# The end of a graph layer on one Trainium2 core: row products split between VectorE and TensorE, eight PSUM banks in two rings, and weights prepared at the start

## The chip, the core and the metric

The kernel runs on one core of a Trainium2 chip. A core has TensorE (matrix products into PSUM, a memory of eight banks), VectorE, ScalarE and GpSimd (work along rows of 128 partitions), SyncE (which issues loads here), and DMA engines that move data between HBM and SBUF. Each engine takes its instructions in order from a queue of its own. The metric is the device time of one execution in microseconds; less is better. Tables of the profile call TensorE PE (PEld where it loads weights), VectorE DVE, ScalarE ACT, GpSimd POOL and SyncE SP.

## The reference, cut to what matters

Four layers follow each other, each with a normalisation. x is 3327 x 64, adj 3327 x 3327. The change touches the end of layer 1 and what it hands to layer 2.

```python
x = _layernorm(x + L0(t, x, adj))        # layer 0
x = _layernorm(x + L1(x, adj, att_W))    # layer 1, in a ball (hyperbolic)
x = _layernorm(x + L2(x, adj, W))        # layer 2
x = _layernorm(x + L3(x, adj, weight, bias))

# layer 1
left, right = x_tan @ att_W[:D] + att_b, x_tan @ att_W[D:]
adj_att = sigmoid(left + right.T) * adj
support = einsum('ij,ijd->id', adj_att, _logmap(x[:, None], x[None, :]))
return _proj(_expmap(x, support))        # per node: norms, tanh, two scalings

# layer 2, twice
agg = adj @ x
x = tanh(concatenate([agg, x], 1) @ W[k])
```

The sum over j in layer 1 can be written as a vector m (a weighted sum of rows of x) and a scalar t (a sum of weights) for each node. What comes after it needs, for each node, three numbers besides scalars that are known early: p, the row product of m with x; q, the squared length of the centred m; and t. The node's result is alpha times m plus beta times x, with alpha and beta worked out from p, q, t by some fifty operations on a tile of 128 x 26 scalars. The product of layer 2 with its first weights is linear, so it is formed as alpha (m W) + beta (x W) once alpha and beta are there.

## The kernel before, in words

Nodes are padded to 26 blocks of 128. A tile "128 x 26" holds one scalar for each node. Columns of nodes are kept turned, two halves of 13 blocks stacked on the 128 partitions (64 features each): `mT` and `ljT` are such tiles of 128 x 1664, and one block of 128 columns stands for two blocks of nodes. Most of the kernel's instructions have an order written out by hand for each engine.

**Beginning (L104 to L300).** SyncE issues the loads in program order: x, the attention weights, two adjacency blocks that stay in SBUF (`keep`, L142 to L146), and then six small loads: layer 2's weights in two halves into `w2_dg`, layer 3's into `w3_dg`, a bias and the attention weights again (L156 to L165). Layer 0 is reduced to a centring and a scaling. In L1267 to L1279 TensorE forms the attention products; after the first and the last group of them a product with no reader (`idle`, L1277) fills its time. ScalarE loads its tables for square root and sigmoid (L1280, L1281).

**Layer 1's loop (`near_sphere`, L1302).** 104 tiles go through products on TensorE (L1400), an arctangent on ScalarE (L1409), two weightings on VectorE (L1420 to L1424), a sigmoid on ScalarE (L1373) times adjacency on GpSimd (L1378), and a product that sums over j into two banks (L1444). ScalarE copies the sums to `mT` (L1450). Before the last tiles end, GpSimd forms the first half of `xm`, the elementwise product of `mT` with the turned rows of x (L1627), and six tiles of scalars (L1630 to L1635); TensorE turns and centres the first six column blocks of `mT` (`pq_early`, L1640), and ScalarE squares them into `sq_e` and copies their t (L1645, L1649). After the loop VectorE makes three tiles of scalars (L1652 to L1654), the other half of `xm` (L1656) and the first 12 of q (L1657).

**Layer 1's end (`near_end`, L1659).** PSUM is divided into a ring of four banks (`l1w`), one bank for p (`l1t`) and a ring of three (`l1m`). TensorE turns and centres the other seven column blocks (`m_and_t`, L1711), then forms p for all 13 blocks as products of `xm` with two columns of ones (`pe`, L1735). ScalarE squares (L1729), VectorE sums (L1773, L1774). ScalarE copies the centred m to `x2` (`m_out`). VectorE works through the scalars: k, gp, u2, th; ScalarE takes tanh (L1819) and loads the table for square roots (L1822); VectorE goes on to `root`, ScalarE takes a root, VectorE goes to `var`, ScalarE takes the second root (L1852, twice); then alpha and beta (L1883, L1884). Meanwhile TensorE works out two weight tiles, `w_x` and `w_m` (L1786 to L1798), turns and centres the first six column blocks a second time, and forms x W (`times(..., w_x, ...)`) and m W (`times(..., w_m, ...)`). Both weight tiles are the centred layer 2 weights with two rows set to zero: `w_x` is made as rows times (center W), `w_m` as (rows times center) W. VectorE combines them into `lj` in five groups (L1890 to L1892), writes the last scalar `beta_c` (shown by the profile as `gsp`, L1893), and finishes `x2` (L1897 to L1899).

**Into layer 2 (L485 to L640).** Loads for it are issued by SyncE in program order: three more kept blocks (L2103) and four stream blocks (L218) before `near_end`, as their buffers come free; then, inside the layer, one block into a buffer `bt` that lies where layer 1's end had its tiles, and further stream blocks. TensorE multiplies `lj` with the adjacency blocks (L517), in the order: four stream blocks, a kept one, `bt`, stream blocks, and so on.

Of the kernel before, what the change touches and what calls it, by code (L numbers as in the profile page):

```python
# [10 lines left out]
F32 = mybir.dt.float32  # L11
# [3 lines left out]
AF = mybir.ActivationFunctionType  # L15
ALU = mybir.AluOpType
# [66 lines left out]
def kernel(  # L83
# [62 lines left out]
    keep((NB - 1, NB - 2))  # L146

# [9 lines left out]
    with nc.allow_non_contiguous_dma(reason="two short columns"):  # L157
# [7 lines left out]
        nc.sync.dma_start(attw_sb, att_w.rearrange("(t d) o -> d (t o)", d=D))  # L165

# [136 lines left out]

    def layer_3_constants():
        nc.gpsimd.tensor_scalar(w3_dg, w3_dg, float(2**27), None, ALU.mult)

    def centred_weights(ps):

        pw = ps.tile([P, P], F32, name="pw_3")
        nc.tensor.matmul(pw, center, w3_dg, start=True, stop=True)  # L310
        nc.scalar.copy(w3_dg, pw)

# [877 lines left out]
    with tc.tile_pool(name="l1", bufs=1) as l1:  # L1190

        def l1_stat(name):
            return l1.tile([P, NB], F32, name=name)

        aa, g1, ga, xn, rxn, gs, gs2, gk, lpn, aav, gsp = (
            l1_stat(name)
            for name in ("aa", "g1", "ga", "xn", "rxn", "gs", "gs2", "gk", "lpn", "aav", "gsp")
# [11 lines left out]
        with tc.tile_pool(name="l1a", bufs=1) as l1a, tc.tile_pool(  # L1209
# [57 lines left out]
            for i, (g, n) in enumerate(turned):  # L1267
# [7 lines left out]
                if i in (0, 3):  # L1275
                    w = 2 if i else 4
                    nc.tensor.matmul(  # L1277
                        idle[:, : w * P], ident, center_4[:, :w], start=True, stop=True
                    )  # L1279
            nc.scalar.activation(root, vq[:, :2], AF.Sqrt)  # L1280
            nc.scalar.activation(warm, ones, AF.Sigmoid)  # L1281
            nc.vector.reciprocal(root, root)
# [19 lines left out]
        def near_sphere(mT, ljT_0, xm, sq_e, t_e):  # L1302
# [3 lines left out]
            with tc.tile_pool(name="n1", bufs=1, reuse_waits="tile") as n1, tc.tile_pool(  # L1306
# [235 lines left out]
                with tc.manual_schedule(  # L1542
# [69 lines left out]
                    for t in range(len(tiles)):  # L1612
# [12 lines left out]
                        if t == len(tiles) - 4:  # L1625
                            of = slice(0, 2 * CW)
                            nc.gpsimd.tensor_tensor(xm[:, of], mT[:, of], riT[:, of], ALU.mult)  # L1627
# [4 lines left out]
                            gp.tensor_scalar(gsp, g1, -0.5, None, ALU.mult)  # L1632
                            gp.tensor_tensor(gsp, gsp, gs, ALU.mult)
                            gp.tensor_tensor(gs2, gs, gs, ALU.mult)
                            gp.tensor_scalar(aav, aa, 1.0 / D, LN_EPS, ALU.mult, ALU.add)  # L1635
                        if t == len(tiles) - 3:
# [15 lines left out]
                    stt(inv_s, vq[:, 1], -0.5 / 0.9, r2[:, 1], op0=ALU.mult, op1=ALU.mult)  # L1652
                    stt(rxn, r2[:, 0], -0.5, inv_s, op0=ALU.mult, op1=ALU.mult)
                    vec(xn, aa, rxn, ALU.mult)  # L1654
                    for of in (slice(c * CW, (c + 1) * CW) for c in (2, 3)):
                        vec(xm[:, of], mT[:, of], riT[:, of], ALU.mult)  # L1656
# [510 lines left out]
```

## Time and profile before

| what | value |
|---|---|
| time, median of three runs | 497.64 us (497.33 to 497.72) |
| profiled execution, whole | 499.74 us |
| profiled execution, span from first to last instruction | 498.0 us |
| granted TensorE clock, mean | 0.981 |
| busy in the span: PE, DVE, ACT, POOL | 480.5, 349.2, 266.3, 196.8 us |
| data read from HBM | 136.93 MB, 277 GB/s over the span |

The profiled execution is one of its own; its time lies 2.1 us above the median of the runs. Every duration and start in this document that is not said to be another's comes from it. By stage (stretch from its start in us; busy time in it):

| stretch | what it is | PE | DVE | ACT | POOL | clock | GB/s |
|---|---|---|---|---|---|---|---|
| 0 to 20 | beginning | 16.92 | 14.34 | 10.36 | 5.71 | 0.87 | 309 |
| 20 to 188 | layer 1's loop | 167.84 | 142.83 | 164.12 | 157.47 | 1.00 | 266 |
| 188 to 206 | layer 1's end | 18.00 | 14.62 | 11.03 | 1.42 | 0.91 | 347 |
| 206 to 226 | layer 2, first blocks | 19.24 | 19.28 | 0.08 | 0.00 | 1.00 | 376 |
| 226 to 300 | layer 2, first pass | 74.00 | 29.16 | 2.19 | 0.00 | 1.00 | 277 |
| 300 to 498 | layer 2's second pass, layer 3 | 184.49 | 128.97 | 78.52 | 32.15 | 0.98 | 273 |

How to read the profile: a group line gives the line of the kernel, the engine, the operation, what it writes and reads with its shapes, how many there are, and in brackets how long the engine was idle before it and what ended that. The chain of waits is followed back from the last instruction: at each step to whatever released it. A float32 product of TensorE appears as two records. Instructions of one engine overlap a little, so starts lie closer together than durations say.

### The profile page before, as it was taken

What the parts mean: (1) busy time and instruction counts of PE and PEld (TensorE: products, weight loads), DVE (VectorE), ACT (ScalarE), POOL (GpSimd) and SP (SyncE); (2) the same over time, 40 slices, a digit from 0 to 9 for tenths busy, and PEclk for the clock granted to TensorE, in tenths of its full rate; (3) what the DMA queues carried; (4) which work ended last, traced back from release to release, by engine and by line L of the source; (5) the groups of instructions that cost most, each with busy time, mean ns of one, the idle gap of its engine ahead of it and who ended that gap; (6) DMA issues with size and microseconds to landing.
All of it is one profiled execution on the core that took longest, in us unless ns stands there. A gap on an engine that the chain in (4) does not pass through costs nothing.

```text
span 498.0 us, 7739 instructions
## 1 busy us (share of the span) xinstructions
PE 480.5 (96%) x2865; PEld 220.6 (44%) x2865; DVE 349.2 (70%) x600; ACT 266.3 (53%) x376; POOL 196.8 (40%) x175
## 2 busy tenths in 40 slices
PE   8999999999999999999999999999999999999991
PEld 4733333333333338643434353333345555555551
DVE  6698888878888887995363322656238999689743
ACT  4799999999999985400000000000016876666641
POOL 4299899989999991000000000000352274000000
PEclk9799999999999998999999999999999999999996
DMA  8988988887888278899999009988987699949001
GB/s 273 379 247 281 328 274 273 272 273 259 280 274 276 77 277 314 372 397 428 424 426 384 0 17 403 427 349 334 421 333 235 222 334 387 365 150 356 17 1 42
DMA packets 34186, 139.20 MB, mean 280 GB/s; under 512 B 11231, under 2 KB 13025, under 8 KB 29019
## 3 DMA queue, kind: packets, MB, share of 16 engines
q1 hardware_dynamic: 30603, 137.41, 73.9%
q0 software_dynamic: 1248, 0.64, 0.6%
q10 hardware_dynamic: 2288, 0.57, 0.6%
q8 instruction: 24, 0.39, 0.3%
q14 instruction: 23, 0.19, 0.1%
HBM read 136.93 MB, written 1.04 MB: 277 GB/s over the span
## 4 chain that ended last, share of the span: by engine, by line
PE 80%; DVE 8%; DMA 5%; issue 1%; ACT 1%; SPq 0%; POOL 0%; DVEq 0%
PE cnt L517 26%; PE pq L1400 17%; PE acc L1444 16%; PE cnt L651 5%; PE acc L883 5%; DMA at_l<-in_adjT 3%; PE acc L900 2%; DMA ah<-in_adjT 2%; PE t L452 2%; DVE mask L368 2%; DVE w L667 1%; PE both L752 1%; PE cnt L508 1%; PE pn_l L403 1%; PE pe L1735 1%
## 5 line engine op out<-in xcount | busy, mean ns | idle before, releaser
L1378 POOL TENSOR_TENSOR sg<-sg,at 128x832 f32<-128x832 f32 x88 | 131.2, 1519 | 7.6 <-ACT sg L1373 3.1
L517 PE MATMUL cnt<-at_l,lj 128*64 128x416 f32 x496 | 90.7, 515 | 0.8 <-DMA at_l<-in_adjT 0.8
L1373 ACT ACTIVATE sg<-lb,rb 128x1664 f32<-128x1664 f32 (+1 forms) x53 | 88.0, 1661 | 0.0
L1400 PE MATMUL pq<-riT,ljT 64*128 64x416 f32 x416 | 87.2, 536 | 0.2
L1444 PE MATMUL acc<-v,lj 128*64 128x416 f32 x416 | 85.1, 525 | 0.0
L1409 ACT ACTIVATE pq<-pq 128x832 f32<-128x832 f32 x104 | 83.8, 850 | 1.7 <-issue 1.6
L630 ACT ACTIVATE x<-cnt 128x416 f32<-128x416 f32 x8 | 4.1, 517 | 144.9 <-PE cnt L517 144.9
L669 ACT ACTIVATE w<-cnt 128x416 int16<-128x416 f32 x135 | 63.9, 520 | 28.3 <-PE cnt L651 26.8
L1424 DVE SCALAR_TENSOR_TENSOR v<-pq,sg 128x832 f32<-128x832 f32 x52 | 53.3, 1025 | 18.7 <-ACT pq L1409 18.3
L464 POOL DMA_DIRECT2D t_rows<-tb x4 | 4.1, 1045 | 151.0 <-DVE tb L462 151.0
L1400 PEld LDWEIGHTS pq<-riT,ljT 64*128 64x128 f32 x416 | 35.6, 186 | 49.5 <-ACT pq L1409 30.6
L517 PEld LDWEIGHTS cnt<-at_l,lj 128*64 128x64 f32 x496 | 34.3, 137 | 50.9 <-issue 48.6
L883 PE MATMUL acc<-w,s 128*128 128x416 bf16 x208 | 53.1, 339 | 0.0
L667 DVE TENSOR_SCALAR w<-cnt 128x416 int16<-128x416 f32 x73 | 42.1, 587 | 10.7 <-PE cnt L651 8.3
L1444 PEld LDWEIGHTS acc<-v,lj 128*64 128x64 f32 x416 | 26.0, 136 | 52.2 <-issue 48.4
L517 PE MATMUL cnt<-kept,lj 128*64 128x416 f32 x224 | 41.6, 514 | 0.0
L651 PE MATMUL cnt<-mask,tri 128*128 128x416 bf16 x136 | 35.6, 339 | 2.1 <-DVE w L667 2.1
L368 DVE TENSOR_SCALAR mask<-ah 128x1664 bf16<-128x1664 f32 x34 | 36.4, 1096 | 1.0 <-DMA ah<-in_adjT 1.0
L1421 DVE SCALAR_TENSOR_TENSOR pq<-pq,sg 128x416 f32<-128x416 f32 x52 | 31.2, 600 | 1.8
L445 DVE TENSOR_SCALAR tm<-at_l 128x1664 bf16<-128x1664 f32 x16 | 15.7, 1023 | 22.8 <-PE t L452 20.9
L1420 DVE SCALAR_TENSOR_TENSOR v<-pq,sg 128x416 f32<-128x416 f32 x52 | 30.2, 580 | 0.0
L1044 POOL DMA_DIRECT2D out<-hid x2 | 1.0, 514 | 73.3 <-DVE hid L1049 73.3
(321 smaller groups left out, 525.6 us busy)
## 6 DMA issues: line engine op xcount, KB each, us to landing
at_l<-in_adjT SPq DMA_DIRECT2D x27, 1664.0 KB, 12.3
at<-in_adjT SPq DMA_DIRECT2D x44, 832.0 KB, 5.8
ah<-in_adjT SPq DMA_DIRECT2D x34, 832.0 KB, 6.6
kept<-in_adjT SPq DMA_DIRECT2D x7, 1664.0 KB, 9.6
bt_l<-in_adjT SPq DMA_DIRECT2D x6, 1664.0 KB
lb<-lf_rows SPq DMA_DIRECT2D x2, 384.0 KB
mask<-t_rows SPq DMA_DIRECT2D x34, 3.2 KB
ljT<-ljT SPq DMA_DIRECT2D x4, 128.0 KB
```

The lines of the kernel that those rows point to most:

```text
L368: nc.vector.tensor_scalar(mask[q], ahead.pop(q), 0.0, None, ALU.not_equal)
L517: nc.tensor.matmul(acc[c][h * D : (h + 1) * D, :], hw[:, slot(jb), :], blocks[jb][:, o : o + CW], start=c not in begun, stop=last, skip_gr ...
L651: nc.tensor.matmul(cnt[c][e], tri, mask[q][:, of], start=True, stop=True, skip_group_check=True,)
L667: nc.vector.tensor_scalar(to, of, 0.0, None, ALU.max)
L669: nc.scalar.activation(to, of, AF.Relu)
L883: nc.tensor.matmul(acc[h, c][:, e, :], s12[:, slot(jb)].rearrange("p t d -> p (t d)"), ws[q, c, e], start=first, stop=last,)
L1373: nc.scalar.activation(sg[:, :, of], lbs[:, :, of], AF.Sigmoid, bias=rb[:, sl : sl + 1])
L1378: nc.gpsimd.tensor_tensor(sg[:, h, of], sg[:, h, of], at[:, h, of], ALU.mult)
L1400: nc.tensor.matmul(pq[:, h, :], ljT[h != jb // NBH][rows, of], riT[rows, ch * CW : (ch + 1) * CW], start=True, stop=True,)
L1409: nc.scalar.activation(pqs[t], pqs[t], AF.Arctan, bias=ANGLE_FIRST, scale=ANGLE_STEP)
L1424: stt(w, pq, ANGLE_REST, sg, op0=ALU.add, op1=ALU.mult)
L1444: nc.tensor.matmul(accs[cp, ci][h * D : (h + 1) * D, :], lj[:, slot(jb), :], w[:, h, :], start=(jb == orders[cp][0]), stop=(jb == orders[c ...
```

## The change

- `keep` for the first two adjacency blocks moves behind the six small loads.
- The filler product after the last group of attention products becomes two products, of `center` with layer 2's first weights and with layer 3's. ScalarE reads them out behind the sigmoid's table load: `w_mean` (rows set to zero) serves for both x W and m W, and `w3_dg` is ready, scaled. What made them in `near_end`, and the two functions that made `w3_dg` in the other branch, go.
- GpSimd no longer forms the first half of `xm`. It makes eleven tiles of scalars where it made six (three come from VectorE; `gmh` stands for `gsp`, `gks` is new), and sums `sq_e` by halves in six additions, which VectorE did in one reduction.
- For the first six column blocks, VectorE multiplies the centred `pq_early` with x, in rows (`xm_e`), and later sums it (`xms`): these are p for 12 of the 26 columns. ScalarE copies the same `pq_early` to `x2`. TensorE does not turn these blocks a second time.
- For the other seven column blocks p is formed on TensorE as before; `xm` is made for these alone.
- Of the last squares, four column blocks are taken as eight operations of 64 columns, each of which also writes its sum (`accum_out`), where VectorE had a reduction.
- PSUM: two rings of four banks, `l1w` for `pm`, `pe` and then m W, `l1x` for x W. TensorE forms x W right behind `pe`, then m W, then two fillers.
- ScalarE copies m and the first x W before tanh, two x W behind the square roots' table load, the last behind the first root.
- The scalars are written with two operations fewer between tanh and the first root: products with tanh are taken out of sums, and the 1 of `ca` and `dn` is added in the operation that reads it.

```diff
-
-    keep((NB - 1, NB - 2))
...
+    keep((NB - 1, NB - 2))
+    w_mean = const.tile([P, P], F32, name="w_mean")
...
-                if i in (0, 3):
-                    w = 2 if i else 4
-                    nc.tensor.matmul(
-                        idle[:, : w * P], ident, center_4[:, :w], start=True, stop=True
-                    )
+                if i == 0:
+                    nc.tensor.matmul(idle, ident, center_4, start=True, stop=True)
+                if i == 3:
+                    for k, w in enumerate((w2_dg[:, 0, :], w3_dg)):
+                        nc.tensor.matmul(
+                            idle[:, k * P : (k + 1) * P], center, w, start=True, stop=True
+                        )
             nc.scalar.activation(root, vq[:, :2], AF.Sqrt)
             nc.scalar.activation(warm, ones, AF.Sigmoid)
+            nc.scalar.activation(w_mean, idle[:, :P], AF.Copy, scale=rows_63)
+            nc.scalar.activation(w3_dg, idle[:, P : 2 * P], AF.Copy, scale=float(2**27))
...
                         if t == len(tiles) - 4:
-                            of = slice(0, 2 * CW)
-                            nc.gpsimd.tensor_tensor(xm[:, of], mT[:, of], riT[:, of], ALU.mult)
...
+                            gp.tensor_tensor(gks, gk, s, ALU.mult)
+                            gp.tensor_scalar(gks, gks, -2.0, None, ALU.mult)
...
+                            w = D
+                            while w > 2:
+                                w //= 2
+                                gp.tensor_tensor(
+                                    sq_e[:, :, :w], sq_e[:, :, :w], sq_e[:, :, w : 2 * w], ALU.add
+                                )
+                            gp.tensor_tensor(lpn[:, :12], sq_e[:, :, 0], sq_e[:, :, 1], ALU.add)
...
+                    vec(first(xm_e), pm[..., :P], first(xc), ALU.mult)
+                    nc.scalar.copy(first(x2), pm[..., :P])
+                    for of in (slice(6 * P, 3 * CW), slice(3 * CW, HALF)):
                         vec(xm[:, of], mT[:, of], riT[:, of], ALU.mult)
-                    nc.vector.tensor_reduce(lpn[:, :12], sq_e, axis=AX.X, op=ALU.add)
...
-                name="l1w", bufs=4, space=PSUM
-            ) as l1w, tc.tile_pool(name="l1t", bufs=1, space=PSUM) as l1t, tc.tile_pool(
-                name="l1m", bufs=3, space=PSUM
-            ) as l1m:
+                name="l1w", bufs=4, space=PSUM
+            ) as l1w, tc.tile_pool(name="l1x", bufs=4, space=PSUM) as l1x:
...
+                def sums_of_squares(g, n):
+                    for k in range(n):
+                        for h in range(2):
+                            sl = 2 * (g + k) + h
+                            nc.scalar.activation(
+                                sqm[:, sl - 12], m_of(g)[:, k, h], AF.Square,
+                                accum_out=q[:, sl : sl + 1],
+                            )
...
+                for g, n in ((6, 3), (9, 3), (12, 1)):
+                    m_and_t(g, n)
+                pe = in_bank("pe")[:, :14].rearrange("p (n h) -> p n h", h=2)
+                for i in range(7):
+                    nc.tensor.matmul(
+                        pe[:, i], xm[:, (6 + i) * P : (7 + i) * P], but_last,
+                        start=True, stop=True,
+                    )
                 vec(gt[:, :12], t_e, gk[:, :12], mul)
                 for g, n in ((6, 3), (9, 3), (12, 1)):
                     t_of(g, n)
+                squares(6, 3)
+                sums_of_squares(9, 3)
+                sums_of_squares(12, 1)
+                nc.vector.tensor_reduce(xms[:, :12], xm_e, axis=AX.X, op=add)
                 nc.vector.tensor_reduce(q[:, 12:18], sqm[:, :6], axis=AX.X, op=add)
-                nc.vector.tensor_reduce(q[:, 18:], sqm[:, 6:], axis=AX.X, op=add)
...
+                xs = {g: in_bank(f"x_w_{g}", l1x) for g in (0, 4, 12, 8)}
+                of_four = dict(fours)
+                for g in xs:
+                    times(xs[g], ljT, w_mean, g, of_four[g])
+
+                vec(k[:, :12], xms[:, :12], gks[:, :12], mul)
+                vec(gta, gt, aa, mul)
+                for g, n in ((6, 3), (9, 3), (12, 1)):
+                    m_out(g, n)
+                x_out(xs[0], *fours[0])
...
+                mw = {b: in_bank(f"m_w_{b}") for b in (0, 3, 1, 2)}
+                for b in mw:
+                    times(mw[b], mT, w_mean, *fours[b])
+                fill = in_bank("fill", l1x)
+                for _ in range(2):
+                    nc.tensor.matmul(fill, ident, center_4, start=True, stop=True)
...
                 nc.scalar.activation(th, arg, AF.Tanh, scale=-1.0)
-                nc.scalar.copy(w_m, second[:, :P])
                 warm_e = st("warm")
                 nc.scalar.activation(warm_e[:, :1], ones, AF.Sqrt)
-                m_out(0, 3)
...
+                x_out(xs[4], *fours[1])
+                x_out(xs[12], *fours[3])
+                ca = both(ux, 2.0, th, "ca", mul, add)
                 be = of(mul, th, g2, "be")
+                e = of(mul, th, u2, "e")
+                vec(ca, ca, th, mul)
+                stt(e, ux, 2.0, e, op0=mul, op1=add)
```

## The prediction

> **What bounds the kernel now.** I read first the granted clock and the span (one core, 498.0 us, clock 0.981), then busy time by stage, then the chain of waits, then every engine's timeline from 185 to 226 us. Layer 1's end lies at 188 to 206 us, between the last pair of its loop and the first product of layer 2 with the adjacency. The chain of waits does not run from there into layer 2 over TensorE. It runs over VectorE, SyncE's queue and a load. Columns: start us, us, what.
>
> ```profile
> 210.01 0.69 DVE lj L1892
> 210.70 0.11 DVE gsp L1893
> ...
> 211.73 0.03 SPq L218
> 211.76 0.03 issue
> 211.79 13.94 DMA at_l<-in_adjT
> 225.73 0.04 issue
> 225.77 5.81 PE cnt L517 x32
> ```
>
> The last scalar of layer 1's end (L1893) ends at 210.8 us. Only then does SyncE issue layer 2's fifth adjacency block. The waits of SyncE's queue name the same pair (us in total, times, longest):
>
> ```profile
> SPq L218 <- DVE gsp L1893: 15.3, 1, 15.3
> SPq L218 <- DVE x L1656: 9.2, 1, 9.2
> ```
>
> That block's buffer lies where layer 1's end has its scalars, so it waits for the last reader of them, and two more blocks queue behind it. TensorE works on four loaded blocks, a kept one and the first two of the queued loads, then waits 0.76 us for the third at 225.77; between 226 and 300 it is busy 74.00 of 74.00 us. So what the change is worth is the time by which **L1893** comes earlier. TensorE's own start into layer 2 (205.23 us) has 0.76 us of slack behind it.
>
> What sets L1893 is a chain on VectorE: the row products `pe`, the scalars, tanh on ScalarE, more scalars, two square roots. Its beginning (start us, us, engine line op, names, [idle before <- releaser]):
>
> ```profile
> 190.86 1.29 DVE L1656 TENSOR_TENSOR x<-mT,riT 128x416 f32<-128x416 f32 x2 [0.83 <-ACT mT L1450]
> 192.06 0.95 DVE L1657 TENSOR_REDUCE lpn<-sq_e 128x12 f32<-128x768 f32 x1
> ...
> 193.46 0.54 DVE L1773 TENSOR_REDUCE lpn<-sq_m 128x6 f32<-128x384 f32 x1
> 193.92 0.67 DVE L1774 TENSOR_REDUCE lpn<-sq_m 128x8 f32<-128x512 f32 x1
> 195.57 0.18 DVE L1781 TENSOR_TENSOR e_k<-pe,gs 128x26 f32<-128x26 f32 x1 [0.98 <-PE pe L1735]
> ```
>
> ```profile
> 190.88 1.86 PE L1715 MATMUL pm<-all_m,mT 128*128 128x130 f32 x14
> 192.57 2.96 PE L1735 MATMUL pe<-but_last,x 128*128 128x2 f32 x26
> ```
>
> VectorE waits 0.98 us for the 13 row products (26 records, 2.96 us, 0.114 us each). These two-column products also cost TensorE its clock: granted 1.00 until 195.7 us, then 0.50 until 199.1 us.
>
> **The change, part by part.**
>
> *Before tanh, VectorE.* Mask sums `t_of` can end at 192.9 us (the last `pm` record ends at 192.74, L1715). The reduction L1657 leaves VectorE for GpSimd, but the new row products of the first 12 columns need one of the same shape: 0.95 us, to 193.85. L1773 stays (0.54, to 194.3). L1774 goes to ScalarE. TensorE now has 7 row products, 14 records by 0.114 us = 1.6 us after 192.74, so `pe` is there at 194.35. The scalars then run at the steps of this trace: 0.10 us between independent ones, 0.22 where one reads its predecessor. From the product with `pe` (194.45): h 0.22, gp 0.10, k 0.10, u2 0.22, ka 0.10, gq 0.10, ux 0.12, u2 0.10, th 0.22, reciprocal 0.22, th·xn 0.35, to tanh 0.22. Sum: 196.5 us against 197.68, a gain of **1.16**. The product `xm_e` (768 from PSUM, about 0.95 by the 1.02 of 832 in L1424) runs at 189.45 to 190.4, where three small operations and a wait of 0.83 stood; the second half of `xm` still ends at 192.15 because it waits for ScalarE's copy of mT (191.53). That matters: the loads of 192.2 us wait for it (L1656, second line of the waits above).
>
> *Before tanh, ScalarE.* Here work is added. The copy of 768 columns into x2 (0.81 by `sq_e`) runs from 191.5 to 192.3, where ScalarE waited 0.79 us. Then one square (0.38 to the next start), eight squares of 64 columns that write a sum each, three copies (1.0) and one of 512 columns (0.5) stand ahead of tanh: 192.3 + 0.38 + 8c + 1.5 = 194.2 + 8c. The trace has no operation with such a sum. A plain one from PSUM would take 0.155 + 64·0.83/1000 = 0.21 and start its successor 0.09 earlier: c = 0.12 if the sum is free. If reading it out is another instruction like a 128x1 ACTIVATE (0.20) and nothing overlaps, c = 0.41. I take 0.31, such an instruction with the overlap of one pair. Tanh then starts at 196.7: a gain of **1.0** (1.16 at c = 0.12, 0.2 at c = 0.41). The same sums are read by gq at 195.3; at c = 0.31 they end at 195.2.
>
> The Trainium skill ("ScalarE: Activation LUTs", What ACT_TABLE_LOAD costs) gives 186 ns + 0.833 ns per element and about 93 ns of overlap, so by it eight plain squares are 1.2 us and tanh comes at the 196.5 of VectorE; it has no price for the sum.
>
> *GpSimd.* It loses the product of 832 columns (1.95, L1627), gets five more small scalars (11 at 0.37, to 189.8), and then adds up `sq_e` by halves, six operations of 384 to 12 columns. By its rows (0.24 for 26 columns, 1.08 for 416, 1.95 for 832) these are 1.0 + 0.6 + 0.4 + 0.3 + 0.26 + 0.24 and gaps of 0.08, 3.3 us: 190.3 to 193.6. gq reads it at 195.3, so it is hidden by 1.7 us; one us of loss begins at twice its length.
>
> The skill speaks against it ("GPSIMD Engine Reference", Engine selection: reduce along the free dimension on VectorE, elementwise work is about 2x slower on GpSimd). By its factor the work is 2 times 0.95 us, hidden as well.
>
> *From tanh to L1893.* From tanh to the first square root the trace has 2.81 us with 22 operations of VectorE. Counted through in the new order (20 operations, the same two steps) it is 2.57: a gain of **0.24**. ScalarE has the table load of 1.28, its first operation 0.20, and copies of 512 and 128 columns (0.5 and 0.3) in these 2.57 us after 0.23 of tanh: 2.4 us, just hidden. Behind the root nothing on VectorE changes, so L1893 moves with it. The products that TensorE delivers are early enough: 13 of x and 13 of m by 0.25 us from 194.35 end at 200.8, two fills (1.1 each by L1277's 512 columns) at 203.0, and layer 2's first product waits for VectorE at 204.50 - 1.2 = 203.3. Should the clock still fall to 0.50 for one stretch of 3.4 us, all this ends near 204 us; layer 2 bears a start up to 204.8 before its wait at 225 is used up.
>
> *Rings.* The four banks of `pm` and `pe` become those of the m products. Each has been read by ScalarE (copies, by 196) before TensorE comes to it at 197.5. `pm_12` and `pe` may lie where `pq_early` was, whose last reader is the new copy (192.3); TensorE comes to it at 192.5. Nothing, or 0.1.
>
> *The beginning.* Two weight products replace a filler of 256 columns (0.68, L1277; now about 1.0) at 13.4 us, and ScalarE gets two readings (0.37 and 0.32 by L1795 and L1778) in its wait of 1.14 us before 15.08. If the turned `lf` products need the bank that they read, these start at 15.1 instead of 14.3 and end at 16.6; TensorE's next work waited until 16.50 anyway. I count **-0.1**. The two kept blocks are issued after six small loads of 0.6 us, at 7.2 instead of 3.6 us; they took 9.6 to 12.8 us to land, GpSimd needs the first at 20.08 and the second at 24.8: hidden, with little to spare.
>
> **Sum.** 1.0 + 0.24 - 0.1 = **1.1 us** off the profiled execution (499.74 us with its surroundings, span 498.0), the same off the median of the three runs, which lies 2.1 lower: 497.64 - 1.1 = **496.5**. All of it must pass the load queue. The loads idle between 210 and 213.5 us (2.5 us of transfer lost), so bringing the issue forward by 1.1 is not eaten by transfers ahead of it.
>
> **Rivals.**
> 1. *ScalarE becomes the bound before tanh.* For it: 8 operations more and four copies moved ahead of tanh; against it: 64 columns are little. With c from 0.36 to its upper end 0.41 the gain is 0.75 down to 0.35: 496.9 to 497.3. No other engine helps, for tanh is behind them in ScalarE's queue.
> 2. *Slower: the weights arrive late at the beginning.* The products stand ahead of the turned `lf` in TensorE's queue and thus ahead of all of layer 1. It decides from a landing at 13.4 us. The last is issued near 6; x took 5.1 us from issue to its first reader, which gives 11. If they take the 9.6 of the kept blocks they land at 15.6, 2.2 us late and 1.1 beyond the gain: 498.7.
> 3. *The gain does not reach the end:* another wait of SyncE's queue, or the load stream, holds the third block at 225.7. Time 497.3 to 497.7.
> 4. *More than counted.* TensorE has 0.50 of its clock at 14.8 to 21.6 us too, with its chain setting the pace there. If the denser work after 14.8 brings the clock back a stretch of 3.4 us earlier, up to 1.5 us more come: 495.0 to 496.
>
> **How the numbers follow.** Forecast (496.1 to 496.8) 0.50, rival 1 0.23, rival 2 0.08, rival 3 0.10, rival 4 0.09. A change of 0.2% (1.0 us) is about what a measurement of this kernel can tell from none. The forecast lies close to that bound: I give four fifths of it to faster, all of rival 4, none of 1 and 3: faster 0.49, same 0.43, slower 0.08. The range goes from half of rival 4 (495.6) over 1 and 3 to the nearer part of 2: 498.2.
>
> **What would show it.** Tanh at 196.5 to 196.7 without an idle ScalarE ahead of it but with VectorE waiting little; `pe` 14 records; L1893 near 209.6; the third load's wait at 224.6, TensorE's wait there longer than 0.76 (its start gains more than the load does); clock at 1.00 through 195.7 to 199.1. Wrong if the eight squares take over 3.3 us, if TensorE idles before 14.3 us at the weights, or if SyncE waits for something other than the last scalar.

## The result, and the profile after

The changed kernel took **501.06 us** (median of 6 runs, 500.44 to 503.13), beside 497.85 us for the kernel before (6 runs, 497.33 to 498.44): a ratio of **1.0057, interval 1.0036 to 1.0077**. Measured again, in `after_again` below, it was 1.0050 [1.0036, 1.0065]. So it is slower by about half a per cent, 2.5 to 2.8 us by these ratios, where 1.1 us of gain were forecast. Its profiled execution took 500.45 us (span 498.6).

The chain that sets the end is the same one. Out of the chain of waits after, and SyncE's queue's waits (us in total, times, longest):

```profile
209.94 0.69 DVE lj L1877
211.72 14.94 DMA at_l<-in_adjT
226.70 5.81 PE cnt L507 x32
```

```profile
SPq L218 <- DVE gmh L1878: 15.4, 1, 15.4
SPq L218 <- DVE x L1665: 9.8, 1, 9.8
```

The last scalar is now L1878 (`gmh`). It ends at 210.73 us, where L1893 ended at 210.80: of 1.24 us of gain forecast for this chain, 0.07 arrived. And behind it the third load takes 14.94 us in place of 13.94, so TensorE goes on at 226.70, not at 225.77. The two profiles differ by 0.7 us only, the timed medians by far more; the experiments on the beginning say what probably hides the rest.

Why the chain gained nothing stands in TensorE's and VectorE's timelines of layer 1's end (start us, us, what, [idle before <- releaser]):

```profile
189.23 1.62 PE L1440 MATMUL acc<-v,lj 128*64 128x416 f32 x8
192.18 1.83 PE L1724 MATMUL pm<-all_m,mT 128*128 128x130 f32 x14 [1.33 <-ACT x L1663]
193.85 1.62 PE L1773 MATMUL pe<-but_last,x 128*128 128x2 f32 x14
```

```profile
190.24 0.96 DVE L1662 TENSOR_TENSOR xm_e<-pq_early,xc 128x768 f32<-128x768 f32 x1 [0.90 <-ACT t_e L1648]
191.11 1.54 DVE L1665 TENSOR_TENSOR x<-mT,riT 128x480 f32<-128x480 f32 x2
```

`pm` starts at 192.18, behind a wait of 1.33 us for the new copy of 768 columns into x2 (L1663); before, it started at 190.88. `pe` has its 14 records, as forecast, but ends 1.1 us later than forecast. On VectorE `xm_e` waits for ScalarE's reading of the same `pq_early` and runs 0.8 us later than forecast, so the second half of `xm` ends at 192.65 in place of 192.15, and the first adjacency loads are issued at 192.74 in place of 192.23.

The beginning after, TensorE:

```profile
13.73 0.78 PE L1271 MATMUL idle<-w_dg,both_m 128*128 128x128 f32 x2
14.30 0.63 PE L1271 MATMUL idle<-both_m 128*128 128x128 f32 x2
15.60 1.94 PE L1455 MATMUL prep_left<-ident,lf 128*128 128x128 f32 x8 [0.67 <-ACT both_m L1277]
17.34 1.06 PE L1477 MATMUL first_right<-ident,lj 128*128 128x128 f32 x4
```

The turned `lf` (`prep_left`) starts at 15.60, before at 14.32: it takes the bank of `idle`, and waits until ScalarE has read the second weight product out of it.

### The profile page after: what moved, and what is told of

Its sections match the earlier page's. It is cut to its first block, busy times and chain, and to the rows that moved or that the text cites. A ratio compares the mean times of both kernels' runs of the same rounds, so it can differ in the third digit from the quotient of the medians.

```text
span 498.6 us, 7708 instructions
## 1 busy us (share of the span) xinstructions
PE 476.9 (96%) x2840; PEld 217.4 (44%) x2840; DVE 350.2 (70%) x597; ACT 266.7 (53%) x386; POOL 198.6 (40%) x185
## 4 chain that ended last, share of the span: by engine, by line
PE 84%; DVE 7%; DMA 3%; issue 1%; ACT 1%; POOL 0%; SPq 0%; ACTq 0%; DVEq 0%
PE cnt L507 26%; PE pq L1396 17%; PE acc L1440 16%; PE cnt L641 7%; PE acc L873 6%; PE acc L890 3%; DMA at_l<-in_adjT 3%; PE t L442 2%; DVE mask L358 2%; PE both L742 1%; PE cnt L498 1%; DVE w L657 1%; PE pn_l L393 1%; PE pr_o L930 1%; DVE lj L1877 1%
```

## The experiments

Each kernel ran beside the kernel before on one chip (not the same chip for all kernels), and ratios are to that. For the end, three numbers are read from each trace: from the end of the loop's last product (`acc`) to the issue of layer 2's third load, from there to its landing, and from the issue of the first load behind the last scalar (`bt`) to that landing.

| kernel | us, median (runs) | ratio [interval] | acc to third issue | issue to landing | bt to landing |
|---|---|---|---|---|---|
| before (first profile) | | | 20.84 | 13.94 | 14.85 |
| before_again | 499.75 (12) | 1.0016 [1.0004, 1.0028] | 20.86 | 14.31 | 15.22 |
| after (first profile) | | | 20.87 | 14.94 | 15.85 |
| after_again | 501.68 (6) | 1.0050 [1.0036, 1.0065] | 20.88 | 14.97 | 15.88 |
| begin_alone | 500.25 (12) | 1.0026 [1.0008, 1.0044] | 21.63 | 13.98 | 15.16 |
| begin_bank | 499.06 (12) | 1.0003 [0.9989, 1.0018] | 20.99 | 14.07 | 15.11 |
| weights_bank | 500.18 (12) | 1.0030 [1.0017, 1.0044] | 20.86 | 14.92 | 15.83 |
| end_alone | 500.21 (12) | 1.0025 [1.0010, 1.0039] | 20.87 | 14.75 | 15.66 |
| own_waits_x | 499.43 (12) | 1.0005 [0.9991, 1.0019] | 20.40 | 14.90 | 15.81 |
| both_fixes | 498.73 (12) | 0.9993 [0.9980, 1.0007] | 19.71 | 15.10 | 16.01 |
| both_again | 498.65 (12) | 0.9994 [0.9980, 1.0008] | 19.72 | 14.77 | 15.68 |
| late_loads | 499.65 (12) | 1.0005 [0.9988, 1.0021] | 21.60 | 13.53 | 15.18 |

The 21.63 us of `begin_alone`, whose end is that of before, contain a longer stretch at half clock (194.9 to 201.8 us).

### Is the kernel before what its first profile showed?

> The kernel before once more, unchanged. Its profiled execution stood 2 us above the median of its own timed runs, and the two profiles differ by 0.7 us where the timed medians differ by 3.2. If that profile was of an unusual execution, this one shows a span near 496 us, the same stages, and where the 2 us lie. If the profiled execution is always 2 us dearer, the span is near 498 again.

The span was 496.4, and most of the 1.6 us lie ahead of the end of layer 1's loop: its last product ends at 189.59 us, in the first profile at 190.95. The granted clock by stage (us, busy times of five engines, clock, DMA share, GB/s), from the first profile of before, then from this one:

```profile
12.20:24.00 11.80, 10.80 (x68) 8.51 (x67) 8.38 (x29) 8.10 (x13) 2.84 (x3) 0.71 1.00 380
```

```profile
12.20:24.00 11.80, 11.59 (x82) 8.71 (x83) 9.46 (x32) 9.17 (x14) 3.66 (x4) 0.86 1.00 371
```

One kernel, clock 0.71 there and 0.86 here: two stretches of 3.41 us at half clock in the first, one in the second. 29 runs of before on this chip lie between 497.45 and 500.50 us, median 499.49. Beside these, the three runs that the forecast was put off (497.64) were low.

### The beginning alone, the end alone

`begin_alone` is before with the move of `keep` and, at the beginning, this (results to a tile that nobody reads):

```diff
+                if i == 3:
+                    for k, w in enumerate((w2_dg[:, 0, :], w3_dg)):
+                        nc.tensor.matmul(
+                            idle[:, k * P : (k + 1) * P], center, w, start=True, stop=True
+                        )
...
+            nc.scalar.activation(w_mean, idle[:, :P], AF.Copy, scale=rows_63)
+            nc.scalar.activation(w_mean, idle[:, P : 2 * P], AF.Copy, scale=float(2**27))
```

> The kernel before with only the beginning of the change: the kept blocks are issued after the small loads, and the weight products and their two readings stand in the first block; the results go to a tile that nobody reads, and layer 1's end is that of before. Theory 1 (the beginning is what costs: the turned lf products wait for the two readings, 1.28 us in the profile after): 1.0 to 2.5 us slower than before. Theory 2 (the ring of layer 1's end costs, the beginning's delay is made good by TensorE's clock): within 0.5 us of before.

`end_alone` is after with these lines taken back and `w_mean = w2_dg[:, 0, :]`.

> The changed kernel with the beginning of before: the kept blocks are issued first, a filler of 256 columns stands in place of the weight products, no readings. It leaves out the centring of layer 2's weights for the products of layer 1's end and that of layer 3's weights, which no other product takes up. Theory 1 (the beginning costs): 0 to 1 us faster than before. Theory 2 (the end costs, by its ring and by the later loads): 1 to 3 us slower than before, the whole of the loss.

Beside the repeat of before (1.0016, which shows what a comparison of equals can give) both halves cost some 0.1% (0.5 us), beside the common median 0.25%. The interval of that repeat, 1.0004 to 1.0028, leaves out 1 although the kernel is the same, so a difference of 0.1 to 0.2% between two kernels proves little by itself. Neither theory had it alone; both were kept.

### Whose bank? The beginning

`begin_bank` is `begin_alone`, and `weights_bank` is after, with one edit (ScalarE's two readings then take `wt` too):

```diff
+                    wt = l1ap.tile([P, 4 * P], F32, tag="pt", bufs=4, name="pt_w")
...
-                            idle[:, k * P : (k + 1) * P], center, w, start=True, stop=True
+                            wt[:, k * P : (k + 1) * P], center, w, start=True, stop=True
```

> The kernel before with only the beginning of the change, the weight products in a bank that nothing needs soon; the results go to a tile that nobody reads. The beginning with the shared bank was 0.5 to 0.8 us slower than before on this chip. If the shared bank is the cause, this one is within 0.4 us of before; if the moved kept blocks or ScalarE's two readings are, it is as slow as with the shared bank.

> The changed kernel with the two weight products in a buffer of the turned x (bank 3) in place of the filler's bank, which the turned lf products take next. If the wait for ScalarE's readings (0.67 us ahead of prep_left, its start 1.28 us later than in before) is the cost of the beginning, prep_left starts near 15.0 instead of 15.6 and the time is 0.6 to 1.3 us below the changed kernel's. If the beginning's loss is made good by the clock, or comes from the kept loads that are issued later, the time stays within 0.4 us.

TensorE in `begin_bank`:

```profile
14.31 0.39 PE L1280 MATMUL pt_w<-both_m 128*128 128x128 f32 x2
14.90 1.80 PE L1464 MATMUL prep_left<-ident,lf 128*128 128x128 f32 x8 [0.21 <-DVE rb L1295]
```

`prep_left` waits for VectorE again, as it did before the change, and no longer for ScalarE. Both pairs moved alike: 1.0026 to 1.0003 and 1.0050 to 1.0030; a third pair, `own_waits_x` and `both_fixes` below, moves from 1.0005 to 0.9993. So the shared bank costs 1.0 to 1.1 us by two pairs and 0.6 by the third, each uncertain by about 1 us; the moved loads, the products and the readings by themselves cost nothing that can be seen. That the profiles of before and after showed no such loss at 22 us is probably the clock: the half stretches ran from 14.8 to 21.6 us in the one, from 13.5 to 20.4 in the other.

The clock may also be how a wait of 0.7 us comes to cost more than that. Over all 20 traces, layer 1's loop begins (its first `pq`) at 21.1 to 22.0 us where the beginning has one stretch of 3.41 us at half clock, at 22.6 to 23.6 where it has two, and at 24.9 where it has three. All six traces with the shared bank have two or three; of the fourteen others, five have one. That is too few to show it.

### What pm waits for: the ring of layer 1's end

`ring_swapped` makes the pool `l1x` ahead of `l1w`, nothing else, so that `pm` and `pe` lie in banks 4 to 7.

> The changed kernel with the two pools of four banks made in the other order, so that the row products pm and pe lie in the four banks that were free, and the x products in those of pq_early. If the ring is what takes the end's gain (pm waits 1.33 us for the copy into x2), pm starts near 190.9 instead of 192.2, tanh and the last scalar come 0.8 to 1.3 us earlier, and the time is 0.8 to 1.3 us below that of the changed kernel. If ScalarE's queue ahead of tanh is the bound, or the load and not its issue sets the third wait of layer 2, pm starts earlier and the time stays within 0.4 us.

It took 506.69 us (5 runs), 1.0166 [1.0140, 1.0192]. TensorE:

```profile
192.32 1.83 PE L1724 MATMUL pm<-all_m,mT 128*128 128x130 f32 x14 [1.33 <-ACT x L1663]
...
201.36 1.88 PE L1810 MATMUL fill<-both_m,ident 128*128 128x512 f32 x4
210.87 5.40 PE L507 MATMUL cnt<-at_l,lj 128*64 128x416 f32 x18 [7.63 <-issue]
```

Both of its theories fell. In banks that are not those of `pq_early`, `pm` still waited 1.33 us for the copy. So it isn't the bank. The reading that fits is that a new pool waits as a whole, for the last use of everything in the pool that it replaces, while the pools of layer 1's loop are made with `reuse_waits="tile"` and wait buffer by buffer. (Before's pools were made like the new ones, but there the last reading of `pq_early` ended at 190.30 us, ahead of `pm`.) And the m products now lay in the banks in which layer 2 begins, which VectorE reads until 210.8: layer 2 started 6.4 us late.

`own_waits_x` gives the two pools waits of their own, and puts `pm` and `pe` at the head of the second ring:

```diff
-                name="l1w", bufs=4, space=PSUM
-            ) as l1w, tc.tile_pool(name="l1x", bufs=4, space=PSUM) as l1x:
+                name="l1w", bufs=4, space=PSUM, reuse_waits="tile"
+            ) as l1w, tc.tile_pool(
+                name="l1x", bufs=4, space=PSUM, reuse_waits="tile"
+            ) as l1x:
...
-                    pm = in_bank(f"pm_{g}")[...]
+                    pm = in_bank(f"pm_{g}", l1x)[...]
...
-                pe = in_bank("pe")[...]
+                pe = in_bank("pe", l1x)[...]
```

> The changed kernel with pools at layer 1's end that wait buffer by buffer, and pm and pe in the second ring ahead of the x products: pm then waits for its own banks and for mT alone. The theory that pm's wait for the copy into x2 (1.33 us) takes the end's gain says: pm starts near 190.8, pe ends near 194.4, tanh and the last scalar come 0.8 to 1.2 us earlier, the third load is issued as much earlier and the time falls by 0.7 to 1.2 us. The rival, that the load stream and not its issue sets layer 2's third wait, says: the last scalar comes earlier and the third load lands within 0.3 us of where it did, the time within 0.4 us.

`both_fixes` has this and the weights' bank; `both_again` repeats it on another chip. Before these, `after_again`:

> The changed kernel once more, unchanged, beside 12 or more runs of before on one chip. On this chip 29 runs of before spread from 497.5 to 500.5 us with a median of 499.5, while the six that gave the verdict had a median of 497.85. If those six were a lucky sample of the clock's position, the ratio here is 1.001 to 1.004. If the change really costs 3 us, it is 1.006 again.

> The two edits before together: the weight products in bank 3 and layer 1's end with pools that wait buffer by buffer. If both waits cost, the time is 1.3 to 2.5 us below that of the changed kernel and so below that of before; if one of them alone, as that one; if neither, within 0.4 us of the changed kernel.

> The kernel with both fixes once more, on one chip with the three that follow. If its 498.73 us (0.9993 of before) was typical, it is 0.998 to 1.001 of before again. If the split kernel's 1.0032 on another chip was typical for both, it is 1.002 to 1.004.

The ratio of the change stands (1.0050), so the loss was no accident of the six runs. The wait is gone; TensorE in `both_fixes`, and its chain:

```profile
190.11 1.62 PE L1441 MATMUL acc<-v,lj 128*64 128x416 f32 x8
191.66 1.86 PE L1727 MATMUL pm<-all_m,mT 128*128 128x130 f32 x14
193.35 1.62 PE L1776 MATMUL pe<-but_last,x 128*128 128x2 f32 x14
```

```profile
211.44 15.10 DMA at_l<-in_adjT
226.58 5.81 PE cnt L507 x32
```

`pm` follows the loop's last product without a gap, in `own_waits_x` too. There and in `ring_swapped` `pm` has the ring made second, so the way the pools wait, and not the banks of `pm`, makes the difference. From the loop's end to the third load's issue `both_fixes` takes 19.71 us, before 20.84: the 1.13 us of gain are there, near the 1.24 forecast. In `own_waits_x` it is 0.44: TensorE had half its clock from 195.0 to 198.4 us in that execution, and ScalarE's copy of x W ahead of tanh waited 0.80 us for it. But the load takes 15.10 us, and the two fixes together only bring the kernel level with before: 0.9993 and 0.9994. The fixes are worth 2.8 us against the change as it was, 1.0 of it at the beginning; of the 1.8 us between `weights_bank` and `both_fixes` the traces show 1.0 to 1.3.

### Where the end's gain goes: three theories that fell

The first theory was the first four loads, issued 1.9 us after the loop's last product in place of 1.3, with GpSimd's additions of `sq_e` by halves (the tree) behind it. `split_first` is `both_fixes` with `xm_e` in two halves, the second behind `xm`; `tree_gate` holds the tree back until `xm` is written; `loads_first` does both (its main lines):

```diff
-                    vec(first(xm_e), pm[..., :P], first(xc), ALU.mult)
+                    early(0)
                     nc.scalar.copy(first(x2), pm[..., :P])
                     for of in (slice(6 * P, 3 * CW), slice(3 * CW, HALF)):
                         vec(xm[:, of], mT[:, of], riT[:, of], ALU.mult)
+                    gp.tensor_copy(lpn[:, 12:13], xm[:, HALF - 1 : HALF])
...
+                    early(1)
```

> Both fixes as before, and the new product xm_e cut in two: its second half is issued after the two halves of xm, which the first four adjacency loads wait for. With both fixes the third load of layer 2 still takes 15.1 us from issue to landing (13.9 in before), and the first four loads are issued 2.0 us after the loop's last product (1.4 in before). If the stream of loads sets layer 2's wait, that is, if the first four loads' later start is what eats the earlier issue, then: the first loads are issued 0.4 to 0.6 us earlier against the loop's end, the third load lands as much earlier, the time falls by 0.3 to 0.7 us, to 0.998 of before or less. If the issue at the last scalar sets it, the time stays or rises by up to 0.4, since VectorE's chain to tanh gets a piece of 0.5 us later.

> Both fixes, and GpSimd's tree of additions waits (by a copy of one column) until VectorE has written the second half of xm. If the tree slows VectorE's products beside it, the two halves of xm take 0.68 and 0.60 us in place of 0.98 and 0.65, the first four loads are issued 0.2 to 0.4 us earlier, and the third load lands as much earlier. If the tree takes nothing from VectorE, the halves stay at 0.98 and 0.65; then the only change is that gq may wait for the tree, which ends near 196.7, and the time rises by up to 0.4 us.

> Both fixes, the tree held back as in the run before, and the second half of xm_e issued after the halves of xm. The theory that the first four loads' start sets the third load's landing: they are issued 1.3 us after the loop's last product, as in before (1.9 with both fixes), the third load lands 0.4 to 0.7 us earlier against the loop's end than with both fixes, and the time falls by as much, to 0.998 of before or less. The rival that the landing is set by the issue at the last scalar: no earlier landing, and the time up to 0.5 us above both fixes, for VectorE's chain gets longer by 0.5.

`split_first`: 500.32 us (11 runs), 1.0032 [1.0017, 1.0047]; the first loads stayed at 1.88 us, since both halves of `xm` now ran beside the tree at 0.98 us each. `tree_gate`: 499.51 (12), 1.0000 [0.9983, 1.0018]; `xm`'s two products in `both_fixes` and in `tree_gate` (ns min/median/max):

```profile
L1666 DVE TENSOR_TENSOR x<-mT,riT x2: 649/815/981, 192.0 to 192.6; 128x480 f32<-128x480 f32 x1, 128x416 f32<-128x416 f32 x1
```

```profile
L1659 DVE TENSOR_TENSOR x<-mT,riT x2: 584/616/649, 191.5 to 192.1; 128x480 f32<-128x480 f32 x1, 128x416 f32<-128x416 f32 x1
```

So the tree does slow VectorE, by 0.33 and 0.07 us. But it doesn't count: `loads_first` issues the first loads after 1.29 us, as before, and is at 499.50 (12), 1.0000 [0.9984, 1.0016], its third load lands 16.00 us after bt. (Why `split_first` stands 1.9 us above `both_fixes` by the ratios is open: its trace lands the third load 0.3 to 0.6 us later, no more. The two ran on different chips.)

The reverse, in the kernel before:

```diff
+                    for _ in range(2):
+                        vec(xm[:, 2 * CW : 3 * CW], mT[:, 2 * CW : 3 * CW], riT[:, 2 * CW : 3 * CW], ALU.mult)
                     for of in (slice(c * CW, (c + 1) * CW) for c in (2, 3)):
```

> The kernel before with the first half of the product xm written three times, so that its second half, for which the first four loads wait, ends some 1.0 us later; VectorE has 0.98 us of waiting for pe behind it to take that up. If the loads' start sets the third load's landing, they are issued 2.3 us after the loop's last product in place of 1.3, the third load lands 0.7 to 1.0 us later though it is issued within 0.2 us of where it was, and the time rises by 0.6 to 1.2 us. If the issue at the last scalar sets it, the landing and the time stay within 0.3 us.

```profile
211.25 1.10 SPq L218
212.46 13.53 DMA at_l<-in_adjT
226.03 5.81 PE cnt L517 x32
```

The first loads were issued 2.35 us after the loop's last product, and the third load still landed 35.13 us after it (before: 34.78 and 35.17). The theory fell in both directions.

The second theory was the fourth load, which waits for TensorE to free a buffer and so comes earlier when TensorE begins layer 2 earlier. `after_fill` adds filler products of 512, 512 and 256 columns to after, `half_fill` of 512 and 256 to `both_fixes`, and nothing else.

> The changed kernel with two and a half filler products of 512 columns more ahead of layer 2, so that TensorE begins it some 0.9 us later; nothing else is touched. If the fourth load takes the third one's share of the queues: the fourth is issued 2.2 to 2.4 us after the third in place of 1.4, the third lands 15.0 to 15.4 us after bt's issue in place of 15.8, and the time falls by 0.4 to 0.8 us although TensorE starts later. If not, the third lands after 15.7 to 16.0 us as before, TensorE waits less for it, and the time stays within 0.3 us.

> Both fixes and one and a half filler products more; TensorE begins layer 2 some 0.6 us later. If the fourth load takes the third one's share: it is issued 2.0 us after the third in place of 1.4, the third lands 15.2 to 15.5 us after bt's issue in place of 15.7 to 16.0, TensorE's wait for it goes from 0.98 us to near nothing, and the time falls by 0.2 to 0.5 us, to 0.9985 of before or less. If not, it lands as late as before, and the time stays within 0.3 us.

501.51 us (6 runs), 1.0066 [1.0048, 1.0085], and 499.60 (12), 1.0016 [1.0002, 1.0031]. The fourth load came 2.10 and 1.86 us after the third in place of 1.43, as intended, and the third landed 15.71 and 15.79 us after bt all the same. TensorE in `after_fill`:

```profile
205.32 11.39 PE L507 MATMUL cnt<-at_l,lj 128*64 128x416 f32 x64
...
222.70 3.01 PE L507 MATMUL cnt<-at_l,lj 128*64 128x416 f32 x16 [0.40 <-DMA at_l<-in_adjT]
226.70 3.02 PE L507 MATMUL cnt<-at_l,lj 128*64 128x416 f32 x16 [0.98 <-DMA at_l<-in_adjT]
```

TensorE starts at 205.32 in place of 204.52 and goes on at 226.70 as before. This theory fell too. (`half_fill` stands 1.1 us above `both_fixes` by the ratios, which neither theory had; its trace, where TensorE goes on 34.7 us after the loop's end as in `both_fixes`, doesn't show why.)

### What the traces show instead: a code packet

From bt's issue to the third landing, the five traces with before's end take 14.85 to 15.22 us, and the fourteen with the new end (all but `ring_swapped`) 15.66 to 16.01. DMA queues (packets, MB, share) of before from 209 to 212 us, and of after from 214 to 219 us:

```profile
q1 hardware_dynamic: 61, 0.60, 59.8%
q8 instruction: 1, 0.02, 2.2%
```

```profile
q1 hardware_dynamic: 172, 2.08, 98.6%
q8 instruction: 1, 0.02, 1.2%
```

There is one packet of code of 16,384 bytes. With before's end it runs between 0.9 us ahead of bt's issue and 0.1 behind it, in the gap of the loads. With the new end it runs 5.4 to 7.4 us behind, under these loads, and takes 0.93 to 0.96 us, where a data packet of 13,312 bytes takes 0.50. These packets seem to follow TensorE's instructions: in layer 1's loop of after, 229 to 273 of its products and weight loads lie between two of them. The new end has some 84 records of products where before's has 111, so it reaches the next packet later. A load has landed when the last of its 16 parts has. In after the first 15 parts are written by 14.33 us after bt's issue and the last at 15.38; in before the last two at 14.34 and 14.45. Over all traces the last part is written at 14.45 to 14.81 with before's end and at 15.19 to 15.59 with the new one. The lag begins where the packet runs: in after, with the packet at 5.5 us, already bt's own load has its last part late (15 parts by 6.41, the last at 7.37); in `both_fixes`, with the packet at 6.6, that load is complete at 6.45, and the next one has the late part (15 by 10.41, the last at 11.54). That is the 0.7 us. It is read from 19 traces of programs with two kinds of ends; no run moved this packet alone, so it is argued and not shown.

### Two more

`keep_early` is `both_fixes` with `keep` where before has it.

> Both fixes, with the two kept blocks issued ahead of the small loads again, as in before. The prediction had them hidden behind the small loads: then the time stays within 0.5 us of both fixes. If the later kept blocks cost at the beginning (their bytes then lie under the first loads of layer 1), the time falls by 0.5 to 1.5 us; if the weights arrive too late behind them for the products at 13.7 us, it rises by 0.5 us or more.

500.15 us (9 runs), 1.0034 [1.0019, 1.0048], against 0.9993 for `both_fixes`, 2 us more. But on the same chip `split_first`, which keeps the change's order of loads, stood at 1.0032, so the times don't settle what the order is worth. The trace shows the wait. TensorE:

```profile
16.46 0.76 PE L1273 MATMUL pt_w<-w_dg,both_m 128*128 128x128 f32 x2 [1.55 <-DMA w_dg<-in_w]
17.62 1.94 PE L1457 MATMUL prep_left<-ident,lf 128*128 128x128 f32 x8
```

The weights arrive late, as the forecast's second rival had it, when the kept blocks go first. The change's move of `keep` avoids that wait; the loop's last product ends at 192.07 us here and at 191.73 in `both_fixes`, each with two stretches at half clock at the beginning.

`end_fixed` is `end_alone` with `own_waits_x` and `xm_e` in halves.

> The beginning of before (kept blocks first, a filler of 256 columns, no weight products or readings), and layer 1's end of the change with pools that wait buffer by buffer and xm_e cut in two. It leaves out the centring of layer 2's weights for the products of layer 1's end and that of layer 3's weights. It shows what the end alone is worth once its wait is gone. By the prediction's sum it would be 1.1 us below before. If the load stream limits it, 0.3 to 0.8 us below before.

499.34 us (12 runs), 1.0015 [1.0001, 1.0028]: 20.26 us from the loop's end to the issue, 14.84 from there to the landing. It has the slow `xm` of `split_first`, and the code packet at 6.35 us behind bt.

No version beats before; `both_fixes` is level with it.

## Why the prediction was wrong, step by step

- **The bound** was right: the last scalar, SyncE's queue, the third load. L1878 releases it, and TensorE's start has slack.
- **Rings: "Nothing, or 0.1" failed.** The step looked at who had last read each bank and found 192.3 us for two of the four tiles (`pm_12`, `pe`). It missed that a pool without waits by buffer holds back its first tile, `pm_6`, for all of them. Price: 1.16 us (20.87 against 19.71 us from the loop's end to the third issue), the whole gain of the end.
- **The beginning: -0.1 failed**, by its size. The condition was named (the bank that they read), its cost set off against TensorE's next work at 16.50. `prep_left` started at 15.60, not 15.1, and the next work at 17.34, without a wait of its own: it stands behind `prep_left` in TensorE's queue, so the slack up to 16.50 was less than the delay. Price: 1.0 to 1.1 us by two pairs of kernels, 0.6 by a third. The kept blocks went out from 8.87 us on, not 7.2; `begin_bank` shows no price for that.
- **"Not eaten by transfers ahead of it" failed**: the load took 0.7 us longer from bt's issue to its landing. By the traces it was not data ahead of it but a code packet beside it; that cause is argued, not shown.
- **The median that the sum was put off** was low: three runs of 497.3 to 497.7, where later sets of 17 to 35 runs of before have medians of 498.6 to 499.5. The profiled execution's own 499.74 was nearer. Beside the six runs that the result itself was compared with (497.85) that is 0.2 us of the miss, beside the later sets 1 to 2; in the ratio it is none.
- **Before tanh, and from tanh on:** right once pm's wait is gone: 1.13 us in `both_fixes` against 1.0 + 0.24. The eight squares cost c = 0.20 each (0.23 and, 0.1 behind it, a separate reading of 0.20), below the 0.31 taken. In `both_fixes` VectorE, not ScalarE, was the later one at tanh, by 0.1 us.
- **"The second half of `xm` still ends at 192.15" failed:** it had VectorE and ScalarE read `pq_early` at once, but `xm_e` started only when ScalarE's readings were done (190.24 for 189.45). `xm` ended at 192.65 and the first loads went out 0.5 us later. `loads_first` and `late_loads` show no price for it.
- **GpSimd**'s additions took 3.55 us against 3.3 forecast, and gq did not wait for them. But it wasn't free: 0.33 us on VectorE's product beside it. The step asked only when the tree ends, not whom it slows.
- **The clock** kept 1.00 at 195.7 to 199.1 us in after, as forecast; it gave nothing, since TensorE was done 1.43 us before layer 2 could start. That the fewer two-column products did it is doubtful: `late_loads` has all 26 records and kept 1.00 there, `own_waits_x` and `keep_early` have 14 and fell to 0.50 for 3.41 us. At the beginning the half stretch that rival 4 saw shortened was as long after as before, 6.83 us. Rival 2, the slower one, named the weights as what could come late; they came in time, and what came late was their reading.

Set against each other: 1.13 gained, 1.16 lost to pm's wait, 1.1 at the beginning, 0.7 to the code packet make 1.8 us slower; 2.5 [1.8, 3.2] were measured in `after_again` and 2.8 [1.8, 3.8] at first. So the sum stands at the lower edge of both intervals, and 0.7 to 1.0 us may have a cause that is not found.

## What to carry to other kernels

When a change makes new pools or tiles at a seam, read the first instruction that uses them as if it waited for everything that the old ones held, and check how their waits are made; put a late reading into a bank that nothing needs next. A gain on a chain that ends in a load is only the load's issue: look what else the DMA engines may carry under it, code too. And take the time that a forecast is put off from many runs, where the clock's stretches move the kernel by more than the change.

## What was not expected of the hardware

- At the beginning and at layer 1's end the time at half clock comes in multiples of 3.41 us, and where it begins differs between executions of one kernel: one, two or three stretches after 12 us (before: 1 and 2; after: 2 and 3), and the loop's last product at 189.59 or 190.95 in before, 190.85 or 192.74 in after.
- A load of 1664 KB had its last part written 0.4 to 1.1 us later in the traces where one code packet of 16,384 bytes ran under it: mostly one part of 16 was late, the others were not.
- TensorE was granted 0.50 of its clock from a point between 194.7 and 196.9 us in four of the five traces with 26 records of two-column products there, and in two of the fifteen with 14; it worked without a gap ahead of that in before. So their number alone does not decide it.
- VectorE's product of two tiles in SBUF took 0.98 us beside GpSimd's additions and 0.65 alone, while `xm_e`, which reads one operand from PSUM, took 0.96 in both. The Trainium skill ("SBUF — State Buffer", Who interferes with whom) says that an instruction of VectorE with two inputs in SBUF contends with a GpSimd instruction that reads SBUF, and one with at most one such input, outside the modes that use two ports, does not; these rows agree with it.
- A square that also writes its sum is two instructions on ScalarE, 0.20 us for both on the average, not 0.41.
